# Decoder layer on one core: the last two query pairs of the first batch projected with seven block products

## The chip, the cores and the metric

The kernel runs on one core of one Trainium2 chip. The metric is the time of one execution on the device in microseconds (us), taken as the median of several runs; lower is better. TensorE multiplies matrices, VectorE (DVE) and ScalarE (ACT) work on rows, GpSimd (POOL) does elementwise work between tiles in SBUF, and SyncE (SP) issues nearly all DMAs here.

## The reference

The input `x` is 4 batches of 512 tokens of 512 numbers. The layer adds three parts, each behind a layer norm: causal attention with 32 query heads and 8 key and value heads of 64, a product with `ctx_2048` whose two sides are rounded to fp8 in blocks, and a mixture of 8 experts with one shared expert. The change touches the projection of the queries alone:

```python
    x = x + _L0_attn_ref(_layernorm(x, axis=-1), L0_attn_wq, L0_attn_wk, L0_attn_wv, L0_attn_wo)
    x = x + _L0_xattn_ref(_layernorm(x, axis=-1), ctx_2048)
    x = x + _L0_ffn_ref(_layernorm(x, axis=-1), ...)
    # inside the attention
    xq = (x @ wq).reshape(Bx, Tx, N_HEAD, HEAD_DIM)
    xq = xq * cos + _rotate_half(xq) * sin
```

## The kernel before

The attention of the four batches runs first, one batch after the other, and the experts follow. A batch has 16 "p" (two query heads that share a key head, 128 rows of transposed queries), grouped in 8 pairs `m` of two p. The main loop (lines 1833 to 1851) walks through score blocks, 20 to a batch. Block n (odd numbers, tiles `sc_n`) holds the scores of a few row tiles: TensorE writes them to four PSUM banks (`scores`, line 1577), DVE adds the mask and takes the row minimum of the negated scores into `pm` and `mn`, and ACT takes the exponential. One block later `turned` (line 1638) transposes `pm` on TensorE into the same four banks (`pt_n`), DVE and ACT copy them to `pT`, and `weighted` (line 1669) multiplies `pT` by the values (`av`). So a `pt` must wait until DVE has read the scores of the block after it out of its bank, and a `sc` until the copies have emptied it.

Between these steps a planner written in the kernel (class `Fill`, line 1430) fills TensorE with other work: projections of queries (`psq`), keys (`psk`) and values (`psv`), output projections (`py`, in seven products in `job_o7`, line 921) and the quantized context. Each job has a due block, a wish date and a cost (`add`, line 1322, called in lines 1327 to 1420; 4 x 860 for a plain projection of one p, 7 x 860 for a pair in seven products). `upto` (line 1488) runs jobs up to a pace; `need` (line 1522) forces a job that a score block is about to read. The planner acts when the program is built: what it leaves is a fixed order on every engine's queue.

A pair of queries is projected in one of two ways.

- `job_q1` (line 730), twice for a pair: four products of 128x512 in one bank, then `rotated` (line 682): DVE multiplies the bank by sin and by cos, four DMAs swap the halves of the sin product (`swap`, line 677, `t2q` to `tsq`), and POOL adds (`t1q<-t1q,tsq`).
- `job_q` (line 741), once for a pair: seven block products (Strassen in Winograd's form), each of two products of 128x256 over k, 14 in all. ACT copies one, DVE adds the others into `t1q` in four instructions, then multiplies the whole pair (128x1024) by sin (`t2q`) and by cos, the same swap in four larger DMAs follows, and POOL adds twice. It needs four sums of token blocks (`job_T`, line 652) and of weight blocks (`job_ws`, line 663).

`WHOLE` (line 420) is the first pair of batch 0 that uses `job_q`. It is 8, so that all eight pairs of batch 0 use `job_q1`, and all 24 pairs of the later batches use `job_q`. POOL forms the weight sums of all eight pairs during batch 0 in either case, in the loaded weights' own tile, and stores them in DRAM (`wsum`) for the later batches; for pairs under `WHOLE` it does so after the plain products have read the weights. The token sums `T_0` of batch 0 are formed too, and nothing reads them.

A wrapper records all instructions, so that every line of the profile says L284; tiles tell them apart.

Of the kernel before, what the change touches and what calls it, by code (L numbers as in the profile page):

```python
# [14 lines left out]
P = 128  # L15
# [293 lines left out]
def decoder_layer(  # L309
# [107 lines left out]
            out=accs[b], in_=xf[b * T : (b + 1) * T, :].rearrange("(i p) d -> p i d", p=P)  # L417
        )

    WB, WHOLE = 2 * P, 8  # L420
    wsums = [dram.tile([P, 7 * WB], F32, name=f"wsum_{m}") for m in range(2 * NG)]

    def load_q(b, m):
# [1899 lines left out]
```

## Time and profile before

| | us |
|---|---|
| runs of the kernel before | 1515.84, 1517.41 (median), 1520.70 |
| the profiled execution, its own time | 1517.71 |
| its span, first to last instruction | 1516.0 |
| busy: PE, PEld (weight loads) | 1491.4, 979.8 |
| busy: DVE, ACT, POOL | 957.8, 606.6, 642.7 |
| score blocks of batch 0, pairs 6 and 7 projected | about 153 to 199 |

The profile is one execution. Its timeline gives start, length, engine, operation, tiles out<-in and count for merged instructions, and in brackets the idle time before with what ended it. A float32 product appears as two records. The ends of PE's records are modelled, so a wait on PE is best seen as the distance between two starts that is longer than the same work takes elsewhere.

### The profile page before, as it was taken

The page shows a single profiled execution, that of the slowest core. Times are in us where ns is not written, and L with a number is a line of the kernel's source. Part 1 is how long each engine was busy: PE and PEld are TensorE (multiplying, and loading weights), DVE is VectorE, ACT ScalarE, POOL GpSimd, SP SyncE. Part 2 cuts the span into 40 slices and gives each one's busy share as a digit, 9 for nine tenths or more (in the row PEclk, how much of TensorE's full clock was granted, in tenths as well). Part 3 has the DMA queues.
Part 4 walks back from the last instruction along what each step waited for, and adds up shares of the span by engine and source line. Part 5 has one row for each costly group of instructions (what it writes and reads, how often), then busy time and mean ns, then how long its engine had stood idle before and what let it go on. Part 6 is the DMA issues. An engine that isn't in the chain of part 4 may idle for free.

```text
span 1516.0 us, 23386 instructions
## 1 busy us (share of the span) xinstructions
PE 1491.4 (98%) x7838; PEld 979.8 (65%) x7841; DVE 957.8 (63%) x2698; ACT 606.6 (40%) x1740; POOL 642.7 (42%) x653
## 2 busy tenths in 40 slices
PE   8999999999999999998999999999999999999999
PEld 5656567776556576655657575655456888878764
DVE  4366865669787667988467788766864554434434
ACT  3554554444455545545654555465111322111100
POOL 2354543242254222344232224333644167767723
PEclk9999999999999999999999999999999999999999
DMA  5575543445252444524245452455061254566526
GB/s 137 163 243 168 167 157 105 122 133 129 83 127 68 146 148 129 159 81 136 70 136 164 137 145 71 140 160 160 23 200 49 98 180 145 164 208 214 202 70 222
DMA packets 120872, 210.74 MB, mean 139 GB/s; under 512 B 16688, under 2 KB 48688, under 8 KB 120240
## 3 DMA queue, kind: packets, MB, share of 16 engines
q1 hardware_dynamic: 116256, 199.03, 43.6%
q0 software_dynamic: 2560, 8.39, 1.6%
q10 hardware_dynamic: 1936, 1.84, 0.4%
q8 instruction: 62, 1.02, 0.3%
q14 instruction: 58, 0.48, 0.1%
HBM read 144.98 MB, written 34.87 MB: 119 GB/s over the span
## 4 chain that ended last, share of the span: by engine, by line
PE 93%; DVE 5%; ACT 1%; issue 1%; DMA 0%; SPq 0%; POOL 0%; DVEq 0%; ACTq 0%; POOLq 0%
PE py L284 14%; PE psq L284 13%; PE sc L284 9%; PE p_s L284 9%; PE p_e L284 9%; PE av L284 9%; PE pt L284 9%; PE ys L284 5%; PE epy L284 5%; PE psv L284 4%; PE psk L284 3%; PE ptr_h L284 1%; DVE pm L284 1%; DVE pT L284 1%; PE spin_a L284 0%
## 5 line engine op out<-in xcount | busy, mean ns | idle before, releaser
L284 ACT ACTIVATE pm<-pm,mn 128x256 f32<-128x256 f32 (+3 forms) x512 | 280.9, 550 | 265.5 <-DVE mn L284 265.4
L284 DVE CUSTOM_DVE_ANT_0 pm<-sc,mask 128x256 f32<-128x256 f32 (+3 forms) x512 | 216.6, 486 | 50.3 <-PE sc L284 50.2
L284 PE MATMUL py<-wo,aT 128*128 128x512 f32 (+1 forms) x608 | 232.8, 519 | 1.3 <-DVE y L284 1.1
L284 POOL TENSOR_TENSOR aT<-aT,rrb 128x512 f32<-128x512 f32 x64 | 82.4, 1301 | 255.0 <-DMA rrb<-rrd 222.9
L284 ACT COPY pT<-pt 128x128 f32<-128x128 f32 (+3 forms) x309 | 126.6, 454 | 145.3 <-PE pt L284 131.1
L284 PE MATMUL sc<-kT,t1q 64*128 64x128 f32 (+3 forms) x1024 | 165.6, 450 | 6.7 <-DVE pT L284 3.0
L284 PEld LDWEIGHTS pt<-ident,pm 128*128 128x128 f32 x1280 | 144.5, 141 | 28.3 <-issue 14.4
L284 PE MATMUL pt<-ident,pm 128*128 128x128 f32 x1280 | 156.4, 274 | 4.0 <-DVE mn L284 3.8
L284 PEld LDWEIGHTS py<-wo,aT 128*128 128x128 f32 x608 | 110.1, 190 | 73.1 <-issue 62.1
L284 PE MATMUL av<-pT,v 128*64 128x512 f32 (+3 forms) x1024 | 152.4, 439 | 0.2 <-ACT pT L284 0.2
L284 DVE COPY pT<-pt 128x128 f32<-128x128 f32 (+3 forms) x203 | 83.6, 439 | 95.5 <-PE pt L284 52.2
L284 POOL TENSOR_TENSOR t1q<-t1q,tsq 128x512 f32<-128x512 f32 x64 | 83.7, 1325 | 139.5 <-DMA tsq<-t2q 100.3
L284 PEld LDWEIGHTS av<-pT,v 128*64 128x64 f32 x1024 | 68.4, 136 | 106.8 <-issue 95.8
L284 PEld LDWEIGHTS sc<-kT,t1q 64*128 64x128 f32 x1024 | 86.4, 188 | 71.8 <-issue 39.4
L284 PE MATMUL psq<-hT,wq 128*128 128x256 f32 (+1 forms) x416 | 131.5, 450 | 1.0 <-DVE acc L284 0.6
L284 POOL TENSOR_TENSOR acc<-acc,y 128x512 f32<-128x512 f32 x64 | 85.3, 1336 | 105.0 <-DVE y L284 100.7
L284 PEld LDWEIGHTS psq<-hT,wq 128*128 128x128 f32 x416 | 76.3, 190 | 38.5 <-issue 28.6
L284 PE MATMUL psq<-T,wq 128*128 128x256 f32 x384 | 95.8, 386 | 2.6 <-ACT t1q L284 2.6
L284 ACT ACTIVATION_READ_ACCUMULATOR pm<-pm,mn 128x1 f32 x512 | 95.6, 187 | 0.0
L284 DVE TENSOR_TENSOR t1q<-psq,t1q 128x512 f32<-128x512 f32 x96 | 60.0, 625 | 47.3 <-PE psq L284 44.1
L284 PE MATMUL ys<-slot_s,gT 128*128 128x512 f32 (+3 forms) x204 | 81.3, 579 | 1.7 <-DVE gT L284 1.7
L284 PE MATMUL p_s<-h3x,slot_s 128*128 128x256 f32 (+1 forms) x232 | 80.7, 483 | 0.0
(243 smaller groups left out, 2341.6 us busy)
## 6 DMA issues: line engine op xcount, KB each, us to landing
wq<-wsum SPq DMA_DIRECT2D x24, 896.0 KB, 5.0
slot_e<-in_L_ffn_W_dram SPq DMA_DIRECT2D x16, 1280.0 KB, 8.8
rrb<-rrd SPq DMA_DIRECT2D x64, 256.0 KB, 4.4
wo<-in_L_attn_wo_dram SPq DMA_DIRECT2D x15, 1024.0 KB, 5.5
tsq<-t2q SPq DMA_DIRECT2D x96, 128.0 KB, 2.6
slot_e<-in_L_ffn_W_dram SPq DMA_DIRECT2D x8, 1408.0 KB, 7.4
kT<-t1k SPq DMA_DIRECT2D x60, 128.0 KB, 3.1
wsum<-wq SPq DMA_DIRECT2D x8, 896.0 KB, 5.3
```

Of the source, the lines that this page charges most:

```text
L284: got = call(*args, **kw)
```

## The change

```diff
-    WB, WHOLE = 2 * P, 8
+    WB, WHOLE = 2 * P, 6
```

Pairs 6 and 7 of batch 0 (p = 12 to 15) are now `job_q` instead of two `job_q1` each. Through `WHOLE` the change also reaches what the planner is told:

```python
                first = [("q1", 2 * m + 1) if m < WHOLE else ("wq", 0, m)] if m else []
                add(5 * m - 10, 0, ("ws", m), job_ws(m), *first, want=5 * m - 10)
...
                add(
                    za + due, MM7, ("q", b, m), job_q(b, m),
                    ("T", b), ("wq", b, m), *([] if b else [("ws", m)]), want=za + want,
                )
```

The weight sums of pairs 6 and 7 follow the load instead of the products, and the pair follows the sums. `last_q` (line 1332), which lets batch 1's token rows take over `hT`, and `scores` (line 1581) name the new jobs.

In the built order the two programs are the same on every engine up to score block 19 of batch 0, and again, apart from a few neighbours that change places near block 97, from block 49 on (batch 1). PE's work between block n and the next, other than scores, transposes and value products, is this (us, counted from the order at the durations of the trace):

| block | 19 | 21 | 23 | 25 | 27 | 29 | 31 | 33 | 35 | 37 |
|---|---|---|---|---|---|---|---|---|---|---|
| before | 9.8 | 6.2 | 0.2 | 9.5 | 9.6 | 6.9 | 7.8 | 7.8 | 7.8 | 8.8 |
| changed | 8.9 | 0.2 | 5.4 | 6.0 | 7.0 | 0.0 | 7.8 | 11.2 | 11.2 | 10.5 |

Pair 6's products stand behind the transposes after block 23 instead of around block 21, and its last one behind block 25. Pair 7's stand behind block 31 instead of blocks 25 and 27. In the changed order PE has, from pair 7 to its first use:

```
pt_30 (16 transposes)
psq_0_7, 14 products
ptr_h_1, 16 transposes of batch 1's rows
sc_33, bank pair 0: reads t1q_0_6
sc_33, bank pair 1: reads t1q_0_7
psk_1_0, psv_1_0, ...
```

## The prediction

> **What bounds the kernel.** I read the page's busy times first, then its chain, then the waits of PE, and then the timeline of the stretch that the change reorders.
>
> ```profile
> span 1516.0 us, 23386 instructions
> PE 1491.4 (98%) x7838; PEld 979.8 (65%) x7841; DVE 957.8 (63%) x2698; ACT 606.6 (40%) x1740; POOL 642.7 (42%) x653
> ...
> PE 93%; DVE 5%; ACT 1%; issue 1%; DMA 0%; SPq 0%; POOL 0%; DVEq 0%; ACTq 0%; POOLq 0%
> ```
>
> PE is busy all the time and the chain that ends last runs through it. So a product less is time less, and a wait of PE is time more, one for one: no slack would absorb it. The chain in order of time prices the two forms of a pair:
>
> ```profile
> 18.93 6.88 PE psq L284 x16
> ...
> 285.76 3.46 PE psq L284 x16
> ```
>
> The first line is a whole pair in the plain form (16 records, eight products of 128x512). The second is eight products of 128x256, 0.432 each; 14 of them are 6.06.
>
> In the stretch that is reordered PE waited only once before, at block 23, where the order gives it 0.2 us of other work:
>
> ```profile
> 171.87 0.40 PE L284 MATMUL ptr_c<-ident_b,qq_c 128*128 128x128 bf16 x4
> 172.94 2.65 PE L284 MATMUL pt<-ident,pm 128*128 128x128 f32 x16 [0.68 <-DVE mn L284]
> 175.69 3.12 PE L284 MATMUL sc<-kT,t1q 64*128 64x512 f32 x12
> 178.74 0.65 PE L284 MATMUL av<-pT,v 128*64 128x512 f32 x2
> ```
>
> From start to start these take 1.07, 2.75 and 3.05. Elsewhere in the same stretch they take 0.22, 1.75 and 1.93. So 2.97 us were lost, and of this only 0.68 is shown as idle. The `pt` waits for DVE to read the scores out of the bank, and DVE is late with quantization work.
>
> **The change part by part.**
>
> *Products.* Two pairs at 6.88 - 6.06: **-1.6 us** on PE. The weight loads rise from 16 to 28 a pair, at 0.19 each; the spacing of 0.216 per record in the line above already holds them, so I add nothing. The Trainium skill, "TensorE: Matmul & The Clock Gate", section "The mechanism", says that a weight load overlaps running matmuls only where the row group differs. All these products use the full array, so by that rule 24 more loads at 0.19 would add 4.6 us and the products would lose 2.9; the spacing speaks against it.
>
> *DVE, ACT, POOL, DMA.* POOL's instructions stay the same in number, since weight and token sums were formed before too. DVE loses four products with rope tables a pair and gains four adds and two wide products, some 2.2 us a pair net; ACT gains 0.37 a pair. On DVE this matters only where PE waits for it, below. SP issues four swaps of 128 KB a pair instead of eight of 64 KB.
>
> *Blocks 21 to 23* lose their cover: the changed order has, after pair 5's last products (2.57), `sc_21` 1.93, `av` 2.30, `pt_20` 1.75, `ptr_c` 0.22, `sc_23` 1.93, `pt_22` 1.75, and no other product: 12.5 from 153.9, so 166.4. DVE has in this order the mins of block 21 (until 161.2, as traced), five copies (2.0), one quantization of four instructions (2.3 alone, 3.8 as traced at 167.17 beside POOL), and the mins of block 23 (2.6), then come PE's last transposes (0.5): 168.6 to 170.1. Loss 2.2 to 3.7; I take 3.3, nearer the traced quantization. Before it was 2.97. **+0.3**, between -0.8 and +0.7. Before and after, the same block starves; the later pair 6 only exchanges the place.
>
> *Blocks 25 to 29.* Let block 25 begin at U. PE without waits: `sc` 1.93, `av` 2.30, pair 6's last product 0.86, two `py` 3.46, `pt_24` 1.75, `py` 1.73, `sc_27`, `av`, `pt_26` 5.98, four `py` and one transpose 7.0: block 29 could begin at U+25.0. Block 29 reads pair 6. DVE's queue up to the sin product of pair 6: the add of the last product, not before U+5.3 (0.6); three row statistics (2.4); three sums of `py` (1.2, 1.2 wide); a copy (0.5); the fourth statistics (0.8); 14 small instructions for batch 1's row root; a `py` sum (0.6), the mins of block 27 (2.7) and six copies of `pt_26` (2.6). The row root is where the rows warn:
>
> ```profile
> 188.49 0.83 DVE L284 TENSOR_SCALAR vea<-mva 128x4 f32<-128x4 f32 x1
> 189.35 1.19 DVE L284 TENSOR_SCALAR rsa<-vea 128x4 int32<-128x4 int32 x1
> 190.57 1.19 DVE L284 TENSOR_SCALAR rsa<-rsa 128x4 int32<-128x4 int32 x1
> 191.67 1.31 DVE L284 TENSOR_SCALAR vea<-vea 128x4 f32<-128x4 f32 x1
> ...
> 194.88 0.16 DVE L284 TENSOR_TENSOR r0a<-r0a,rsa 128x4 f32<-128x4 f32 x1
> ```
>
> ```profile
> 189.23 2.51 POOL L284 TENSOR_TENSOR aT<-aT 128x512 f32<-128x512 f32 x2
> 191.67 1.29 POOL L284 TENSOR_TENSOR wo<-wo 128x512 f32<-128x512 f32 x1
> ```
>
> Beside POOL's sums for the output projection each small instruction ends where a POOL instruction ends, and all 14 take 6.94 (188.49 to 195.43); alone they would take 14 x 0.19 = 2.7. Before, this lay beside 3.5 us of pair 7's and `py` products that stood ahead of the transposes. In the changed order POOL's four sums follow `py` at U+12.1, DVE reaches the root at U+12.0, and `pt_26` stands right behind `av`. So the root ends at U+18.9, the sin product begins at U+24.8, and the way from there through swap and POOL is the next fence's, 7.2: block 29 begins at U+32.0. **+6.9**; +2.7 if the root runs alone, +8.5 if it ends 1.8 after POOL's last weight sum, as traced. Part of it falls on `pt_26`, the rest on `sc_29`.
>
> *Block 33.* Pair 7's products now stand right ahead of the block that reads them. The fastest of the 24 pairs in the trace of before:
>
> ```profile
> 968.87 0.69 DVE L284 TENSOR_TENSOR t1q<-psq,t1q 128x512 f32<-128x512 f32 x1 [1.04 <-PE psq L284]
> 969.59 1.23 DVE L284 TENSOR_TENSOR t2q<-t1q,rt 128x1024 f32<-128x1024 f32 x1
> 970.88 2.74 SPq L284 DMA_DIRECT2D tsq<-t2q  x4
> 975.53 2.50 POOL L284 TENSOR_TENSOR t1q<-t1q,tsq 128x512 f32<-128x512 f32 x2 [6.26 <-DMA tsq<-t2q]
> ```
>
> Its last product ended at 968.83; the first of POOL's two adds ended at 976.80: 8.0 us through add, sin product, four DMAs and POOL. In the changed order PE has 16 transposes (1.75) and half of `sc_33` (0.86) in between, of which some 0.2 lies under the last record's end: 2.4. Nothing stands on DVE between add and product, so I take 8.0: **+5.5**. Queued behind the waiting score on PE is everything, batch 1's projections first. Pairs whose DMAs or POOL add stood behind others took up to 13 (two such pairs: 12.6 and 13.1), which would make it +10.4; a little faster DMAs, +5.0. SP has a 896 KB weight load issued just ahead of the swap.
>
> *After block 33* the order holds 11 us of other work a block instead of 8, where before PE did not wait anyway, so nothing is given back. From block 49 the order is as before.
>
> Sum: -1.6 + 0.3 + 6.9 + 5.5 = **+11.1**. On the profiled execution's 1517.7 (span 1516.0 and 1.7 around it) that is 1528.8; that execution lies 0.3 above the median of the runs, so I put **1528.5**. Bounds: -1.6 - 0.8 + 2.7 + 5.0 = +5.3 (1522.7) and -1.6 + 0.7 + 8.5 + 10.4 = +18.0 (1535.4).
>
> **Rivals.**
>
> 1. *POOL and the row root miss each other*, by DVE reaching it one or two us earlier, and block 27 costs 2.7 instead of 6.9: +6.9, 1524.3. For: POOL is idle for 0.8 us just before. Against: before, they met with the same neighbours.
> 2. *The swap is late*: the weight load ahead of it fills the DMA queues and block 33 costs 9 to 10: +15, 1532.5. For: transfers behind such loads were slow in two of 24 pairs. Against: PE has left that load's buffer 2 us before the sin product ends.
> 3. *Not slower: the lost time comes back later.* While PE waits at block 33, DVE, ACT and POOL finish their queues; PE's waits in 410 to 441 (3.5 before a `psq`, 1.1 to 2.7 before several `pt` and `sc`, some 10 in all, all for DVE and ACT) would shrink by this lead. From 6.6 us recovered on it is within 0.3% of before, and with all 10 it is 1518.5. Against: between 216 and 408 PE never waits, so those engines wait for PE there and a lead has no place to be kept.
> 4. *Only the products count*: pair 7's way is under 2.4 and DVE is never late: 1515.8. None of 24 pairs was under 8.0.
>
> **How the numbers follow.** Forecast 0.60, rival 1 0.20, rival 2 0.10, rival 3 0.05, rival 4 0.05. The range, 1521.5 to 1535, holds the first three with their bounds. A difference under 0.3% (4.6 us, so 1512.9 to 1522.0) can't be told from no change here. Slower by more: forecast, rival 2 and nearly all of rival 1, 0.89; faster by more: 0.01; within it the rest, 0.10.
>
> **What would show it.** PE's product time falls by 1.6. In the changed profile the second half of `sc_33` waits some 5.5 us for POOL's `t1q` (nothing waited for that before); `pt_26` and `sc_29` start 7 us late in sum, with the small instructions of the row root stretched to 1.2 each; the wait at block 23 stays near 3. From 300 us on both traces run in parallel, shifted by the whole difference. I am wrong if block 33's scores begin within 3 us of pair 7's last product, or if the shift at 300 us is not the shift at the end.

## The result and the profile after

The changed kernel took **1536.15 us** (median of 4 runs, 1528.75 to 1538.29) against 1517.76 of the kernel before on the same chip: ratio **1.0107, 95% interval 1.0087 to 1.0127**. Taken again later (e11) it was 1532.97 (4 runs, 1531.82 to 1533.77), with 1517.41 for the kernel before beside it: ratio 1.0100, interval 1.0085 to 1.0115. The prediction was 1528.5, 1521.5 to 1535. Slower was right, and the places were right; the size was too small by 4 to 7 us, and the first median lies just over the upper end of the range.

The page of the changed kernel (profiled execution 1535.42 us):

```profile
span 1533.7 us, 23443 instructions
...
PE 1496.6 (98%) x7865; PEld 990.1 (65%) x7865; DVE 966.8 (63%) x2709; ACT 603.2 (39%) x1735; POOL 642.8 (42%) x653
...
PE 91%; DVE 6%; ACT 1%; DMA 1%; SPq 1%; issue 1%; POOL 0%; DVEq 0%; POOLq 0%; ACTq 0%
```

The span is 17.7 longer, PE's busy time only 5.2, though its products should take 1.6 less. The other 12.5 is idle time. PE's waits between 150 and 260 us (total, times, longest) name for whom:

```profile
PE pt L284 <- DVE mn L284: 7.4, 2, 4.9
PE sc L284 <- POOL t1q L284: 6.1, 2, 5.8
```

The second row did not exist before. The timeline of PE shows the places; distances between starts count, since waits are shown only in part:

```profile
162.32 2.10 PE L284 MATMUL sc<-kT,t1q 64*128 64x512 f32 x12
...
166.98 3.43 PE L284 MATMUL pt<-ident,pm 128*128 128x128 f32 x16 [2.56 <-DVE mn L284]
170.21 0.63 PE L284 MATMUL ptr_c<-ident_b,qq_c 128*128 128x128 bf16 x4
...
176.11 1.99 PE L284 MATMUL sc<-kT,t1q 64*128 64x512 f32 x12
...
190.25 2.37 PE L284 MATMUL av<-pT,v 128*64 128x512 f32 x16
197.50 3.68 PE L284 MATMUL pt<-ident,pm 128*128 128x128 f32 x16 [4.88 <-DVE mn L284]
...
208.82 2.00 PE L284 MATMUL sc<-kT,t1q 64*128 64x128 f32 x12 [0.33 <-POOL t1q L284]
...
229.00 1.13 PE L284 MATMUL sc<-kT,t1q 64*128 64x512 f32 x4
235.93 2.08 PE L284 MATMUL sc<-kT,t1q 64*128 64x128 f32 x8 [5.79 <-POOL t1q L284]
237.94 4.30 PE L284 MATMUL psk<-hT,wk 128*128 128x512 f32 x8
```

The first three lines are block 23, 176.11 is the U of the prediction, 208.82 is block 29, and 229.00 and 235.93 are the halves of block 33. DVE and POOL ahead of the wait of 4.88 show the row root of batch 1:

```profile
188.63 1.20 DVE L284 TENSOR_SCALAR vea<-mva 128x4 f32<-128x4 f32 x1
189.87 1.19 DVE L284 TENSOR_SCALAR rsa<-vea 128x4 int32<-128x4 int32 x1
191.09 1.19 DVE L284 TENSOR_SCALAR rsa<-rsa 128x4 int32<-128x4 int32 x1
...
196.00 0.16 DVE L284 SCALAR_TENSOR_TENSOR sha<-mva,rsa 128x4 f32<-128x4 f32 x1
```

```profile
188.54 1.26 POOL L284 TENSOR_TENSOR wo<-wo 128x512 f32<-128x512 f32 x1 [0.94 <-PE py L284]
189.76 2.50 POOL L284 TENSOR_TENSOR aT<-aT 128x512 f32<-128x512 f32 x2
192.22 1.26 POOL L284 TENSOR_TENSOR wo<-wo 128x512 f32<-128x512 f32 x1
```

Each of the first small instructions ends with an instruction of POOL (189.83 with 189.80; 191.06 and 192.28 with the two of 189.76), while the last, behind POOL's run of sums, takes 0.16. The 14 take 7.5 us, as they had taken 6.9 before beside the same neighbours. The main difference is what PE has to do meanwhile. That POOL causes the stretching is read from these ends; no run took POOL's sums away.

What the prediction did not contain is in the table by windows (us, busy time of PE, PEld, DVE, ACT and POOL, PE's granted clock, DMA). Three stretches after the waits ran at half clock; before, the whole reordered stretch ran at full clock.

```profile
167.50:170.90 3.40, 3.40 (x19) 3.25 (x18) 3.39 (x17) 3.38 (x13) 3.32 (x5) 0.50 0.23 95
...
194.80:201.60 6.80, 4.09 (x18) 4.01 (x19) 6.59 (x26) 4.54 (x14) 0.16 (x1) 0.50 0.01 4
...
232.40:239.20 6.80, 3.27 (x10) 1.68 (x11) 1.16 (x7) 1.04 (x5) 4.51 (x4) 0.50 0.12 30
```

So there are two theories for the experiments. **A**: the loss is late data at the three places, and the half clock is a small consequence. **C**: the half clock is most of it. From the starts of the scores in two traces one can read by how much the way between two blocks grew against before; this table carries the verdicts, but for e5 and e6, whose orders differ more (us, last column the reordered stretch as a whole). The order up to block 19 is the same in all of them, and still block 19 stands up to 3 us earlier or later than before from one execution to the next (-2.8 in e7, +3.1 in e8), so medians alone can't decide about 1 or 2 us.

| kernel | 19 to 25 | 25 to 29 | 29 to 33 | 33 to 35 | 35 to 49 | 19 to 49 |
|---|---|---|---|---|---|---|
| changed | +1.06 | +0.02 | -6.84 | +11.05 | +9.40 | +14.69 |
| changed, again | -1.06 | -0.01 | -6.83 | +12.41 | +9.40 | +13.91 |
| e1, short row root | -1.19 | -5.12 | -6.83 | +12.20 | +9.41 | +8.47 |
| e2, pair 7 without rotation | -1.19 | +0.42 | -6.77 | +3.44 | +9.40 | +5.30 |
| e3, both | -1.18 | -5.14 | -6.83 | +3.44 | +9.40 | -0.31 |
| e4, dummies at three places | -0.01 | +8.90 | -6.83 | +10.30 | +9.40 | +21.76 |
| e7, dummies in block 33 | -1.19 | -0.08 | -6.82 | +9.45 | +9.40 | +10.76 |
| e8, dummies ahead of pt_26 | -0.70 | +0.01 | -6.83 | +12.45 | +9.40 | +14.33 |
| e9, swap ahead of the load | -1.19 | -0.07 | -6.83 | +10.07 | +9.41 | +11.39 |
| e10, e7 and e9 together | -1.19 | +0.37 | -6.76 | +8.60 | +9.40 | +10.42 |

The columns 29 to 33 and 35 to 49 hold only work that the change moved from one side to the other; they are alike everywhere. The other three are where the kernels differ.

### The profile page after: what moved, and what is told of

Its sections match the earlier page's. It is cut to its first block, busy times and chain, and to the rows that moved or that the text cites. A ratio compares the mean times of both kernels' runs of the same rounds, so it can differ in the third digit from the quotient of the medians.

```text
span 1533.7 us, 23443 instructions
## 1 busy us (share of the span) xinstructions
PE 1496.6 (98%) x7865; PEld 990.1 (65%) x7865; DVE 966.8 (63%) x2709; ACT 603.2 (39%) x1735; POOL 642.8 (42%) x653
## 4 chain that ended last, share of the span: by engine, by line
PE 91%; DVE 6%; ACT 1%; DMA 1%; SPq 1%; issue 1%; POOL 0%; DVEq 0%; POOLq 0%; ACTq 0%
PE py L284 13%; PE psq L284 13%; PE p_s L284 9%; PE p_e L284 9%; PE sc L284 9%; PE av L284 9%; PE pt L284 9%; PE ys L284 5%; PE epy L284 5%; PE psv L284 3%; PE psk L284 3%; PE ptr_h L284 1%; DVE pm L284 1%; DVE pT L284 1%; SPq L284 1%
## 5 line engine op out<-in xcount | busy, mean ns | idle before, releaser
L284 POOL TENSOR_TENSOR aT<-aT,rrb 128x512 f32<-128x512 f32 x64 | 84.3, 1332 | 241.3 <-DMA rrb<-rrd 197.0
L284 ACT COPY pT<-pt 128x512 f32<-128x512 f32 (+3 forms) x302 | 123.1, 454 | 144.4 <-PE pt L284 130.5
L284 PE MATMUL pt<-ident,pm 128*128 128x128 f32 x1280 | 159.9, 279 | 10.7 <-DVE mn L284 10.5
L284 PEld LDWEIGHTS pt<-ident,pm 128*128 128x128 f32 x1280 | 148.0, 144 | 33.9 <-DVE mn L284 15.6
L284 PE MATMUL psq<-hT,wq 128*128 128x256 f32 (+1 forms) x408 | 123.4, 435 | 0.6 <-DVE acc L284 0.6
L284 PE MATMUL psq<-T,wq 128*128 128x256 f32 x416 | 102.9, 385 | 2.6 <-ACT t1q L284 2.6
L284 DVE TENSOR_TENSOR t1q<-psq,t1q 128x512 f32<-128x512 f32 x104 | 64.9, 624 | 60.4 <-PE psq L284 56.2
L284 PEld LDWEIGHTS psq<-T,wq 128*128 128x128 f32 x416 | 77.1, 191 | 14.6 <-ACT t1q L284 3.0
```

The lines of the kernel that those rows point to most:

```text
L284: got = call(*args, **kw)
```

## The experiments

**e1: the row root of batch 1 in 2 VectorE instructions instead of 14**: this one and the last of the 14, which gives `sha`; those between are left out.

```diff
-        nc.vector.tensor_scalar_add(ve, mv[:, :, 1], LN_EPS)
+        tc.nc.vector.tensor_scalar_add(rs, mv[:, :, 1], LN_EPS)
...
```

> The changed kernel in the same order on every engine, but batch 1's row root is two VectorE instructions instead of 14 (the inverse root is replaced by variance plus eps, so batch 1's rows are scaled a little wrongly). Theory A (late data: PE waits because the operands of three blocks come late, each by a way of its own, and the clock is halved after long waits): the mins of block 27 begin some 5 us earlier, the 4.9 us wait of pt_26 falls under 1, block 29 begins 4 to 6.5 us earlier, and the span falls from 1533.7 to about 1527.5 to 1529.5. Rival B (the seven-product form itself costs, through its adds and copies on DVE and ACT): no change beyond 1 us. Rival C (not the waits but the half clock that follows costs most): 1 to 2 us, and only if the half-clock window near 195 us goes.

Measured: 1529.56 (1527.41 to 1531.78), ratio 1.0071, interval 1.0051 to 1.0092. The wait ahead of `pt_26` is gone and block 29 begins at U+27.6 (U is 175.08) instead of U+32.7:

```profile
189.22 2.38 PE L284 MATMUL av<-pT,v 128*64 128x512 f32 x16
191.53 2.40 PE L284 MATMUL pt<-ident,pm 128*128 128x128 f32 x16
...
202.65 2.00 PE L284 MATMUL sc<-kT,t1q 64*128 64x128 f32 x12 [1.00 <-POOL t1q L284]
```

The stretched row root holds back 5.1 us. The two instructions left take 2.4 us (187.60 to 190.02), near the 2.7 that the prediction gave to a root alone, and block 29 still stands 2.6 behind the U+25.0 of a PE without waits. Block 33 waits as before.

**e2: pair 7 of the first batch without its rotation** (the lines left out, for this pair alone).

```diff
-        nc.vector.tensor_tensor(R2, Xp, rot(1), ALU.mult)
-        nc.vector.tensor_tensor(Xp, Xp, rot(0), ALU.mult)
-        swap(ts, R2)
-            gpsimd(Xp[:, i, :], Xp[:, i, :], ts[:, i, :], ALU.add)
```

> The changed kernel in the same order, but pair 7 of batch 0 is left without its rotation (two wide VectorE products, four swap DMAs and two GpSimd adds are left out), so its scores can read it right after the last add. Theory A: the 5.8 us wait inside sc_33 goes, and with it the half clock after it (1.6 us at sc_33 and the key projection): the span falls by 6 to 7.7 us, to about 1526 to 1528. Rival B: the fall is that of the removed VectorE instructions at most, 0 to 2.5 us. Rival C: the wait goes but the span falls by about 2.

Measured: 1523.98 (10 runs, 1519.38 to 1527.08), ratio 1.0038, interval 1.0026 to 1.0051. Block 33 costs 7.6 us less in the table than in the first profile of the changed kernel, which is the expected size (9.0 less than in the repeat); its scores run through in one group of 12, and the first key product follows 1.92 after their start. The 3.44 that are left are the work that the order moved there (11.2 instead of 7.8). The medians differ by 12.2, more than expected: the first median of the changed kernel is high by itself (below). Against the repeat's 1532.97 it is 9.0.

**e3: both left out.**

> Both cuts in one kernel (short root of batch 1, no rotation of pair 7). Theory A: the two add up, 10 to 14 us less than the changed kernel, a span of 1520 to 1524; what is left over the kernel before is the wait around block 23 and the rest of pair 6's way, less 1.6 us of products. If the second wait only moves where the first was removed (the data of pair 7 late for another reason): clearly less than the sum of the two. Rival B: under 3 us.

Measured: 1519.66 (10 runs, 1516.78 to 1522.79), ratio **1.0010**, interval 1.0000 to 1.0021. The two parts add up: the stretch is 0.3 shorter than before instead of 14.7 longer, and 5.2 + 7.6 = 12.8 of the difference of 15.0 are these two columns (the rest, 2.2, is block 23, below). Hardly anything of the loss is left without the row root and the rotation of pair 7.

**e4: transposes of the identity as dummies in the three waits**, to keep PE's clock up (theory C; the calls alone, `busy` is a loop of transposes).

```diff
+        busy({22: 18, 26: 36}.get(n, 0))      # in turned(), ahead of the transposes
+            if c and n in (33,): busy(46)     # in scores(), between the halves
```

> The changed kernel in the same order, with dummy transposes put into PE's three long waits (18 ahead of pt_22, 36 ahead of pt_26, 46 between the halves of sc_33), each a little shorter than the wait. Theory A with the clock as an effect of the waits: the waits stay, the half-clock windows near 168, 195 and 232 us don't come, and the span falls by 2 to 4.5 us. Rival C: the span falls by 8 or more. If the granted clock has nothing to do with PE's idle time: no change, and windows as before.

Measured: 1539.08 (4 runs, 1535.85 to 1540.96), ratio 1.0132, interval 1.0110 to 1.0153. At `pt_26` the dummies stood in the wrong bank. They went to that of `av`, which ACT empties only after the exponentials of block 27, and these wait for the same VectorE queue:

```profile
189.87 2.37 PE L284 MATMUL av<-pT,v 128*64 128x512 f32 x16
200.73 6.66 PE L1564 MATMUL busy<-ident 128*128 128x128 f32 x36 [8.48 <-ACT aT L284]
```

So they began when the real work could have begun, and cost 8.9. It tells nothing of the clock at that place. The 18 at block 23 overran its wait (`pt_22` begins 4.67 after `sc_23`, in the repeat 3.62), and those in block 33 kept the clock full, with 1.42 of the wait left. e7 and e8 ask again, one place each.

**e5: only pair 7 in seven products** (`WHOLE = 7`).

> Only pair 7 of batch 0 in seven products (the constant at 7). The built order puts 8.6 us of other PE work between pair 7's products and block 33, against 2.6 in the changed kernel, and pair 6 stands where it stood before. Theory A: no wait inside sc_33 (its way takes 8.0 to 8.7), no late block 29, 0.8 us less in products, a wait at block 27's transposes like the changed kernel's since they too stand right behind av: between the two kernels, +2 to +7 us over before. Rival B (the form costs by the pair): half of the changed kernel's loss, +8 to +9, without a place where PE waits longer than 2 us.

Measured: 1523.94 (8 runs, 1523.42 to 1528.66), ratio 1.0042, interval 1.0029 to 1.0056. In its order no `sc` waits for POOL any more, since 10 us lie between pair 7's last product and block 33; the row root still meets POOL (8.8 us from first to last), and the `pt` behind it waits 5.5 for DVE. The loss of 6.0 on the medians lies within what A expected, and that wait is where it arises: in the profiled execution, the slowest of the eight, the stretch is 7.7 longer, with 6.8 us of half clock behind that wait.

**e6: the change, with the wish dates of the pairs of batch 0 three blocks earlier.**

```diff
-                    ("T", b), ("wq", b, m), *([] if b else [("ws", m)]), want=za + want,
+                    ("T", b), ("wq", b, m), *([] if b else [("ws", m)]), want=za + want - 3 * (not b),
```

> Both pairs in seven products, but the planner's wish dates of batch 0's pairs lie three blocks earlier. In the built order pair 6's products stand behind block 25 and pair 7's behind block 27, two blocks (over 25 us of PE work) ahead of their first scores, and every block from 25 on has 5 us or more of other work. Theory A: no wait of PE for t1q at all; the span lies within 5 us of the kernel before, 1514 to 1521. Rival B: both pairs still pay their form, +10 or more over before.

Measured: 1520.60 (10 runs, 1518.43 to 1526.49), ratio **1.0025**, interval 1.0008 to 1.0042. The same seven products for the same two pairs, only elsewhere in the order, and three quarters of the loss are gone. Pair 7's last product ends at 211.97 and block 33 begins at 240.36, so the rotation is hidden. The row root is stretched here too (193.07 to 199.50), but PE has `py`, `sc` and `av` beside it, and waits 1.75:

```profile
201.44 3.62 PE L284 MATMUL pt<-ident,pm 128*128 128x128 f32 x16 [1.75 <-DVE mn L284]
...
240.36 2.00 PE L284 MATMUL sc<-kT,t1q 64*128 64x512 f32 x12
```

So the product form does not itself cost by the pair, which was rival B of the expectations. It is the best version with these products, and not better than the kernel before: its interval lies above 1, and the 1.6 us of products saved are not seen in it.

**e7: dummies only between the halves of block 33.**

> The changed kernel with 46 transposes of the identity (0.11 each, 5.1 us) on TensorE between the two halves of the scores of block 33, where it waits 5.8 us for pair 7; nothing else changed. The earlier trial with three such places lost its meaning at block 27, because its transposes were given the bank that ScalarE empties after that block's own work, and so waited themselves for 8.5 us. Theory A (the loss is late data, the half clock only its consequence, worth 0.94 + 0.71 = 1.65 us at this place): the window of half clock at 232 disappears, the second half of the scores takes 1.07 from start to start instead of 2.01 and the first key product 3.43 instead of 4.14, the data come as late as before, so the way from block 33 to block 35 shortens by at most 1.65 us and the kernel stays above 1531. Rival C (the half clock is most of the loss): the kernel falls by 4 us or more. Rival D (the transposes cost as much as they save, for instance by running over the arrival of the data): the way from block 33 to 35 is within 0.5 us of the changed kernel.

Measured: 1531.22 (4 runs, 1526.01 to 1533.41), ratio 1.0088, interval 1.0071 to 1.0105. No half clock near 232; the data come as late as before, and the work behind them is fast:

```profile
225.55 5.24 PE L1564 MATMUL busy<-ident 128*128 128x128 f32 x46
231.37 1.14 PE L284 MATMUL sc<-kT,t1q 64*128 64x128 f32 x8 [0.58 <-POOL t1q L284]
232.44 3.70 PE L284 MATMUL psk<-hT,wk 128*128 128x512 f32 x8
```

The second half takes 1.07 instead of 2.01, the way from 33 to 35 shortens by 1.6, as A had it (by 3.0 against the repeat). The intervals of the two ratios overlap, so the medians can't tell 1.6 us apart; the trace can.

**e8: dummies only ahead of `pt_26`**, now in a bank that is free (`mm`, whichever came free first).

> The changed kernel with 42 transposes of the identity (4.6 us) ahead of the transposes of block 26, where TensorE waits 4.9 us, now written to the product bank that came free first, which VectorE has left by then; nothing else changed. Theory A: the transposes run at once, the half clock window at 195 to 202 disappears or shortens, the transposes of block 26 take 1.75 from start to start instead of 3.47 and start when they started before; VectorE, not the clock, sets the date of block 29, because the way from the mins of block 27 through the sin product and the swap does not run on TensorE: block 29 moves by less than 1 us and the kernel stays within 2 us of the changed one. Rival C: block 29 moves by 1.7 us or more, and the kernel with it.

Measured: 1532.30 (4 runs, 1528.87 to 1539.12), ratio 1.0083, interval 1.0066 to 1.0100.

```profile
194.56 4.81 PE L1564 MATMUL busy<-ident 128*128 128x128 f32 x42
199.53 2.57 PE L284 MATMUL pt<-ident,pm 128*128 128x128 f32 x16 [0.17 <-DVE mn L284]
...
210.81 2.00 PE L284 MATMUL sc<-kT,t1q 64*128 64x128 f32 x12 [1.00 <-POOL t1q L284]
```

The window of half clock at 195 is gone and `pt_26` takes 2.41 instead of 3.47 to the next start, but block 29 stands where it stood (20.49 after block 27, against 20.50): what PE gained became a longer wait for POOL, 1.00 instead of 0.33. At this place the half clock costs nothing, since VectorE sets the date; in e2 and e10, where its window reached further behind `pt_26` and no wait for POOL was left at block 29, it cost 0.4 (+0.42 and +0.37 in the table). That speaks against C.

**e9: the swaps of pair 7 issued ahead of the weight load** on SyncE, all else in the same order.

```diff
-            bulk(out=w.rearrange("p s k n -> p (s k n)"), in_=wsums[m])
+            late.append(dict(out=w.rearrange("p s k n -> p (s k n)"), in_=wsums[m]))
...
         swap(ts, R2)
+        tc.nc.sync.dma_start(**late.pop())
```

> The changed kernel with one exchange on SyncE: the four swaps of pair 7 are issued ahead of the 896 KB weight load of the second batch, which stood ahead of them; all else in the same order. Rival 2 of the prediction in small (the load delays the swap): VectorE's sin product to POOL's first add comes down from 5.4 us after its end to the 4.4 to 4.5 that other pairs show, the wait at block 33 from 5.8 to 4.8, and the kernel by 1 us, too little for the medians, but to be read in the trace. If the load does not matter, the wait stays at 5.8.

Measured: 1531.01 (4 runs, 1526.61 to 1531.22), ratio 1.0073, interval 1.0053 to 1.0093. SyncE and POOL in the changed kernel, then in e9:

```profile
227.23 0.34 SPq L284 DMA_DIRECT2D wq<-wsum  x1
229.21 2.47 SPq L284 DMA_DIRECT2D tsq<-t2q  x4
```

```profile
234.61 2.48 POOL L284 TENSOR_TENSOR t1q<-t1q,tsq 128x512 f32<-128x512 f32 x2 [10.67 <-DMA tsq<-t2q]
```

```profile
226.97 2.47 SPq L284 DMA_DIRECT2D tsq<-t2q  x4
229.55 0.52 SPq L813 DMA_DIRECT2D wq<-wsum  x1
```

```profile
231.47 2.48 POOL L284 TENSOR_TENSOR t1q<-t1q,tsq 128x512 f32<-128x512 f32 x2 [8.79 <-DMA tsq<-t2q]
```

From the first swap's issue to POOL's start it is 5.40 with the load ahead and 4.50 without; the wait of block 33 falls from 5.79 to 4.89. e10 has 4.49 without; with the load ahead four other executions have 5.34 to 5.47, and e4 6.20. The load costs **0.9 us**.

**e10: e9 with 40 dummies in block 33.**

> The changed kernel with the swaps of pair 7 ahead of the weight load and 40 transposes of the identity (4.4 us) between the halves of the scores of block 33. If the two costs of that block are separate, as theory A has it, both gains are had: the wait with the transposes in it ends 4.9 us after the first half, as with the swap first alone, no half clock follows, and the way from block 33 to block 35 is 22.7 - 1.0 - 1.6 = 20.1 us. The kernel is then some 2.6 us under the changed one of the same chip. If they are one cost told twice, the way stays at 21.1 or more.

Measured: 1530.78 (6 runs, 1527.79 to 1536.49), ratio 1.0093, interval 1.0076 to 1.0111. The way from 33 to 35 is 20.24, expected 20.1: the load and the clock are two costs, and both can be had back. The median is 2.2 under that of the changed kernel beside it; the intervals of the two ratios overlap.

**e11: the changed kernel again.**

> The changed kernel itself once more, nothing edited, for two questions. First, its median beside those of the variants on one chip. Second, block 23: in its first profile the transposes of block 22 waited 2.56 us, with VectorE's last quantization instruction taking 1.63 us beside GpSimd, where four variants that have the same order up to there waited 1.40 with 0.69. If that was the chance of one execution, this profile shows 1.40 again, no half clock at 168, and a span some 2 us shorter (1531.5); if the changed kernel is different there for a reason of its own, it shows 2.56 again.

Measured: 1532.97 (4 runs, 1531.82 to 1533.77), ratio 1.0100, interval 1.0085 to 1.0115, span 1531.8. Block 23 waited 1.41, with full clock behind it:

```profile
168.12 2.65 PE L284 MATMUL pt<-ident,pm 128*128 128x128 f32 x16 [1.41 <-DVE mn L284]
...
235.91 2.08 PE L284 MATMUL sc<-kT,t1q 64*128 64x128 f32 x8 [5.75 <-POOL t1q L284]
237.93 5.71 PE L284 MATMUL psk<-hT,wk 128*128 128x512 f32 x8
243.47 1.89 PE L284 MATMUL psv<-wv,hT 128*128 128x256 f32 x8
```

So the 2.56 of the first profile was chance in that execution: there one quantization instruction of VectorE began after POOL's `aT` (164.50 to 167.45) and took 1.63 us, here it began before POOL's (166.77 and 166.95) and took 0.69. Six other traces have the 1.40 of this one. VectorE's timeline in the first profile, then in this one:

```profile
164.68 1.63 DVE L284 TENSOR_TENSOR qq_c<-qv_c,qm_c 128x512 bf16<-128x512 f32 x1
```

```profile
166.77 0.69 DVE L284 TENSOR_TENSOR qq_c<-qv_c,qm_c 128x512 bf16<-128x512 f32 x1
```

On the other hand `psk` behind the wait of block 33 took 5.54 to the next start here and 4.14 in the first profile, against 3.53 at full clock. The same wait costs 1.5 or 3.0 us more by where the windows of half clock fall: from the second half of block 33 to block 35 it is 14.22 at full clock (e7 and e10 alike), 15.76 in the first profile, 17.18 in this one.

## Why the prediction was right in place and too small in size

- **Products, -1.6.** Right: a pair in seven products takes 6.04 in the repeat (221.02 to 227.06), predicted 6.06. The added weight loads cost nothing that shows, against the 4.6 that the rule cited in the prediction would give.
- **Blocks 21 to 23, +0.3.** The loss was put at 3.3. It was 4.4 in the first profile (4.66 - 1.93 for `sc`, 3.23 - 1.75 for `pt`, 0.2 for `ptr_c`) and 2.4 in the repeat. The mechanism held, and whether VectorE's quantization meets POOL differs between executions: +1.4 or, in most, -0.5. The 4.4 lies over the prediction's bound of 3.7; that 3.3 lies between the two is luck.
- **Blocks 25 to 29, +6.9.** Right in mechanism, and nearly in size: block 29 at U+32.7 both times, predicted U+32.0, so +7.7 over the U+25.0 without waits (32.0 gives 7.0; the 6.9 is rounded). VectorE reached the row root at U+12.5 instead of 12.0 and needed 7.5 instead of 6.9; the sin product began at U+25.8 (24.8); the way to POOL's sum was 6.9 (7.2). Rival 1, root and POOL missing each other, did not happen; e1, whose root takes about as long as one alone, shows what it would have been worth: 5.1, where the rival had 4.2.
- **Block 33, +5.5: the term that was too small.** The mechanism was right: nothing else waits there, and e2 removes the whole cost. The size was 7.6 to 9.0. The data came 8.67 after the last product instead of 8.0 (0.9 of it the weight load ahead of the swap, e9; without it the way is 7.78, in e9 and e10 alike), so PE waited 6.1. And a wait of that length is followed by half clock, another 1.5 or 3.0, of which the prediction had no term. Rival 2 named the load and priced it at 4 us more; it is real and worth 0.9. That its 1532.5 is nearest to the repeat's median is luck, since most of what the forecast lacked came from elsewhere.
- **After block 33, no lead given back, but no fixed shift either.** Rival 3 did not happen: in the first profile the shift against before stays at 14.0 from block 49 to block 81. In the repeat it falls from 15.4 to 13.8 at block 61, but by the clock. All traces wait 2.56 for a `psq` there; the kernel before had half clock behind it (first fence, 3.41 us long), and the repeat had none (second fence):

```profile
415.32 2.73 PE L284 MATMUL psq<-T,wq 128*128 128x256 f32 x8 [2.56 <-ACT t1q L284]
416.50:419.80 3.30, 3.30 (x16) 2.78 (x15) 1.40 (x3) 0.69 (x2) 2.17 (x2) 0.50 0.84 183
```

```profile
430.76 1.99 PE L284 MATMUL psq<-T,wq 128*128 128x256 f32 x8 [2.56 <-ACT t1q L284]
431.90:435.20 3.30, 3.30 (x27) 3.05 (x27) 2.10 (x5) 2.00 (x5) 1.79 (x2) 1.00 0.90 184
```

Later, from block 83 to 107, the first profile lost another 1.9 us and the repeat 2.0, and behind the last score block 1.8 and nothing. So 3.7 and 0.3 came in all behind block 49. The prediction had named this as a sign of being wrong (the shift at 300 us is not the shift at the end), and in that part it was: it had no term for the clock. These later losses go with half clock. Twelve traces have another order than before. The eight with half clock near 700 to 720 lose 0.7 to 3.5 between blocks 83 and 107, the other four (e4, e7, e9, e10) -0.5 to 0.3. The six with half clock near 1105 to 1121 lose 1.4 to 2.8 behind the last score block, the others at most 0.4. The trace of before has waits of 2.56 and 1.75 at these two places, with full clock behind them. What makes the half clock come and go was not tried, and one trace of the kernel before can't say whether the change makes it more frequent.
- **The sum.** First profile: -1.6 + 1.4 + 7.7 + 6.1 + 1.5 = 15.1 against 14.7 in the stretch, which with 3.7 behind it and -0.7 ahead of it make the 17.7 of the span. Repeat: -1.6 - 0.5 + 7.7 + 6.1 + 3.0 = 14.7 against 13.9, which with 0.3 behind it and 1.5 ahead of it make the 15.8 of its span; 0.4 and 0.8 are not accounted for. Predicted were 11.1. (Its upper sum, 18.0, is near what was measured, but held a way of some 13 us at block 33, which did not come.) Of the 3 to 4 us that the prediction lacks in the stretch, the clock behind block 33 is the largest part.

e1, e2 and e3 take away a wait together with the half clock behind it, so they show the places; e7 and e8 part the two. Theory A stands for the two large places and C falls at `pt_26` (e8). But A called the clock small throughout, and at block 33 it is 1.5 to 3.0 of some 8 us, which is not small.

## What to carry to other kernels

A product form that saves 0.8 us a pair on a full engine is paid with a longer way from the last product to the data's reader; before counting the saving, look what stands between the two in the new order (here 2.4 us of work over a way of 8), and whether an earlier place would hide it (e6 lost a quarter of what the change lost). Price a long wait on TensorE with what follows it, not only with its length. A filler for such a wait must write to a bank that is free already, or it waits for the same queue and makes matters worse (e4).

## What was not expected of the hardware

TensorE's granted clock falls to half in stretches of 3.4, 6.8 or 10.2 us behind waits. In the traces here, in the reordered stretch: waits of 1.40 at block 23 (seven traces) were followed by none, one of 1.75 (e6) and one of 2.56 by 3.4 us, those of 4.9 by 3.4 or 6.8 us, those of 5.5 to 5.9 by 6.8 us, and the 8.48 of e4 by 10.2 us. The length of the wait does not decide alone: further on, the same wait of 2.56 for a `psq` (415 to 437 us) has half clock beginning with it or at most 1.5 us after it in eight of the 13 traces, and the same wait of 1.75 near 1100 to 1120 has it at most 2.1 us after in six. Dummy transposes that leave 0.2 to 0.6 us of the wait, and 1.4 in e4, keep the clock full. The Trainium skill, "TensorE: Matmul & The Clock Gate", section "What's actually happening", says that the clock drops to half after at least one idle window of about 3.4 us, and that the windows run freely, not from the kernel's start. The lengths, all multiples of 3.4, and the change from execution to execution agree with that; the waits of 2.56 and 1.75 are shorter than the window it names, and still were followed by half clock in some executions.

The half clock counts only where PE sets the date: 1.5 to 3.0 us at block 33 (e7 and e10 against the two profiles of the changed kernel), nothing at `pt_26` where VectorE was later than PE either way (e8).
